# Slot tiles of a mixture-of-experts stage: probability folded into the rows, a fused ReLU and sum, more transposes by DMA, rows loaded further ahead

## The chip, the cores and the metric

The kernel runs on one core of one Trainium2 chip, as one launch. The time is the device time in microseconds; what is compared is the median over runs of the same program.

## What is computed

The input is 2 x 2048 rows of 512 float32 features. Two layers follow, each with a residual: cross-attention to 128 context rows and a quantised feed-forward in the first; a second cross-attention and a mixture of experts in the second. Only the last part is touched by the change:

```python
def _L1_ffn_ref(x, Wg, bg, We, be):      # x: layer-normalised rows
    probs = jax.nn.softmax(x @ Wg + bg, axis=-1)          # 512 columns
    idx = jnp.argmax(probs, axis=-1)
    p = jnp.take_along_axis(probs, idx[..., None], axis=-1)[..., 0]
    e_idx = idx % We.shape[0]                              # one of 8 experts
    h = jax.nn.relu(jnp.einsum('bsd,edf->besf', x, We) + be[None, :, None, :])
    onehot = jax.nn.one_hot(e_idx, We.shape[0], dtype=x.dtype)
    out = jnp.einsum('besf,bse->bsf', h, onehot) * p[..., None]
    return out
...
    x = x + _L1_ffn_ref(_layernorm(x, axis=-1), ...)
```

Each row goes to one expert, is multiplied with that expert's 512 x 512 weights, passes a ReLU, is scaled by its probability p and added to the row it came from. Since p is positive, p times the ReLU of a value is the ReLU of p times the value.

## The kernel before

The 4096 rows are 32 tiles of 128. The second layer runs a software pipeline over the tiles, `for n in range(NT)`: scores, exponentials, mixing, projection, then the gate's logits and the pick of an expert (`logits`, `picked`, `gated`, two tiles behind). `gated` leaves in each row of `xw[n]`, besides the 512 features, four columns: the mean (column D), the inverse deviation (D+1), the probability (D+2, written at L1008) and a zero (D+3). Then it writes the whole row to `x_dram`.

For the experts the rows are sorted: `routing` counts how many rows go to each expert and gives every row a place in a slot tile, 128 rows that all belong to one expert. There are 39 slot tiles. The first routing covers the first 22 row tiles and makes slot tiles 0 to 14; the second covers the rest and makes 15 to 38. `routing` is a generator whose steps are spread between other work. The second has eleven steps: one with three small products on TensorE, three of small VectorE work (the fourth the longest), two that make one-hot tables, four VectorE products of 128 x 1024 (L1124), and a last one in which TensorE sums 32 products (L1132) and VectorE turns the sums into row numbers (up to L1138).

For slot tile j, `expert(j)` does in order: start the indirect gather of tile j+4 on GpSimd (`gathered`, L1149, into one of six row buffers); turn tile j+1 (`turned_x2`); the matmuls with the expert's weights, which a register picks (L1185); normalise tile j+3 (`centered_x`, VectorE, L104); ReLU times p on ScalarE (L1188); add the row on VectorE (L1189); indirect scatter to the output on GpSimd (L1190).

There are two ways to turn a tile. On TensorE: four transposes into PSUM (L116), then a ScalarE copy that adds RAISE to one row through a bias (L1175). By DMA: VectorE adds RAISE to four columns (L1161), splits the float32 words into 16-bit halves (L826), a DMA on SP's queue transposes them (L829), and ScalarE joins the halves (`joined`, L832). RAISE carries the expert's bias into the product, since the weights hold the bias divided accordingly. Before, the odd tiles from 5 on go by DMA, 17 of 39.

From the second layer on, the order on TensorE, VectorE, ScalarE and GpSimd is the order of the program text; each engine runs its list strictly in turn. Slot tiles 0 and 1 run within the last two rounds of the attention loop, 2 to 4 between the last gate steps, 5 to 38 in the last loop, into which the steps of the second routing are woven for the first of them. PSUM tiles of the tag "m" have four buffers. All scatters write to the same output tensor.

Buffers of the slot stage are old row tiles seen through `part(n, ...)`.

Of the kernel before, what the change touches and what calls it, by code (L numbers as in the profile page):

```python
# [16 lines left out]
U16 = mybir.dt.uint16  # L17
I8 = mybir.dt.int8
AF = mybir.ActivationFunctionType
# [44 lines left out]
def two_layers(ctx: ExitStack, tc: tile.TileContext, a, out):  # L64
# [38 lines left out]
    def center(dst, x, mean, scale):  # L103
        nc.vector.tensor_scalar(dst, x, mean, scale, ALU.subtract, ALU.mult)  # L104
# [720 lines left out]
    def split(x, planes):  # L825
        nc.vector.tensor_copy(  # L826
            planes.rearrange("p (h f) -> p h f", h=2), x.bitcast(U16).rearrange("p (f h) -> p h f", h=2)
        )
        nc.sync.dma_start(out=x.bitcast(U16).rearrange("p (b q) -> p b q", q=P), in_=planes, transpose=True)  # L829

    def joined(dst, x):
        nc.scalar.copy(  # L832
            dst.bitcast(U16).rearrange("p c (q h) -> p h c q", h=2),
            x.bitcast(U16).rearrange("p (h c q) -> p h c q", h=2, c=ND),
        )
# [181 lines left out]
    def part(n, shape, dtype=F32, at=0):  # L1017

        size = math.prod(shape)
        v = xw[n][:, at : at + (size * mybir.dt.size(dtype) + 3) // 4]  # L1020
        if dtype is not F32:
            v = v.bitcast(dtype)[:, :size]
        if len(shape) == 1:
            return v
        names = "abc"[: len(shape)]
        return v.rearrange(f"p ({' '.join(names)}) -> p {' '.join(names)}", **dict(zip(names, shape)))
# [120 lines left out]
    def gathered(j):  # L1147
        if j < NJ:
# [2 lines left out]
                in_offset=bass.IndirectOffsetOnAxis(ap=tile_of[j][2], axis=0),  # L1151
            )

    def centered_x(j):
        if j < NJ:
            x = xw[j % 6]
            xn = part(6 + j % 3, [D])
            center(xn, x[:, :D], x[:, D : D + 1], x[:, D + 1 : D + 2])
            if by_dma(j):
                first = xn.rearrange("p (c q) -> p c q", c=ND)[:, :, 0:1]  # L1160
                nc.vector.tensor_scalar(first, first, RAISE, None, ALU.add)  # L1161
                split(xn, part(24 + j // 2 % 2, [2 * D], U16))

    def by_dma(j):

        return j > 4 and j % 2 == 1

    def turned_x2(j):
        if j < NJ and by_dma(j):
            ring[j] = part(9 + j % 3, [ND, P])  # L1170
            joined(ring[j], part(6 + j % 3, [D]))
        elif j < NJ:
            pt = transposed(psm, part(6 + j % 3, [D]))
            ring[j] = part(9 + j % 3, [ND, P])
            nc.scalar.activation(ring[j], pt, AF.Identity, bias=raised)  # L1175

    def expert(j):

        te, tok, _ = tile_of[j]
        gathered(j + 4)  # L1180
        turned_x2(j + 1)
        e = nc.tensor.value_load(te, min_val=0, max_val=NE - 1)
        pz = psm.tile([P, D], F32, name="pz", tag="m")
        for c in range(ND):
            nc.tensor.matmul(pz, ring[j][:, c, :], we[:, bass.ds(e, 1), c, :], start=(c == 0), stop=(c == ND - 1))  # L1185
        centered_x(j + 3)
        x, acc = xw[j % 6], part(12 + j % 3, [D])
        nc.scalar.activation(acc, pz, AF.Relu, scale=x[:, D + 2 : D + 3])  # L1188
        nc.vector.tensor_tensor(acc, acc, x[:, :D], ALU.add)  # L1189
        nc.gpsimd.indirect_dma_start(  # L1190
            out=out_rows, out_offset=bass.IndirectOffsetOnAxis(ap=tok, axis=0),
            in_=acc, in_offset=None, bounds_check=NT * P - 1, oob_is_err=False,
        )
# [32 lines left out]
    for n in range(NT):  # L1226
        blk, t = n // NB1, n % NB1
        ahead = blk + 1 < nblk
        fs = range(t * ND // NB1, (t + 1) * ND // NB1)
        if n > 0:  # L1230
            biased(n - 1)
        firsts = [m for m in (n + 2 * NB1, n + 2 * NB1 + 1) if m < NT and (m >= TURNED) == (m > n + 2 * NB1)]
        firsts = [normed(m) for m in firsts]
        scores(n)
        if 4 <= n < 4 + 2 * NE and n % 2 == 0:

            nc.scalar.dma_start(out=rowadd, in_=v_dram[(n - 4) // 2].partition_broadcast(P))

        late = t == 0 and n > 1
        if ahead and not late:  # L1240
            queries(blk + 1, fs[:1])
        if late:
            logits(n - 2)
        exponentials(n)
        if ahead and late:
            queries(blk + 1, fs[:1])
        if n == 0:
            for i in range(NT - held, NT - held + 2):
                down(i)
                widened(i + 2)  # L1250
        shares(n, 0)
        if n > 1:
            if not late:
                logits(n - 2)
            picked(n - 2)
        shares(n, 1)
        if n > 0:
            projected(n - 1)
            normed2(n - 1)()
        firsts = [first() for first in firsts]  # L1260
        rest = gated(n - 2) if n > 1 else None
        if n + 1 < NT:
            kept_keys(n + 1)
        for first in firsts:
            if first:
                first()
        if 0 < n <= NE:
            load(we[:, n - 1], a["L1_ffn_We"][n - 1].rearrange("(c p) f -> p c f", p=P))
        if ahead:
            queries(blk + 1, fs[1:])  # L1270
        if n == 0:
            for i in range(NT - held + 2, NT):
                down(i)
            dwn.close()
            ffd.close()
            moe = ctx.enter_context(tc.tile_pool(name="moe", bufs=1, side="right"))
            we = moe.tile([P, NE, ND, D], F32, name="we")
        if 4 <= n < 4 + 2 * NE:
            e, half = divmod(n - 4, 2)
            for c in range(2 * half, 2 * half + 2):  # L1280
                nc.gpsimd.tensor_tensor(we[:, e, c, :], we[:, e, c, :], rowadd, ALU.add)
        if not ahead:

            expert(n - NT + NB1)
        turned(n)
        if rest:
            rest()
        if n > 0:
            turned2(n - 1)
        mixed(n)  # L1290
        if t == NB1 - 1 and blk + 2 < nblk:
            for t in range(NB1):
                turned1((blk + 2) * NB1 + t)
        if n == NTA + 2:
            route = routing(True)
        if route:
            for _ in range(3 if n == NTA + 2 else 2):
                if next(route, route) is route:
                    route = None
                    for j in range(4):  # L1300
                        gathered(j)
                    break
        if n == NT - NB1 - 1:
            for j in range(3):
                centered_x(j)
            turned_x2(0)
    biased(NT - 1)
# [11 lines left out]
    expert(4)  # L1319
    route = routing(False)  # L1320
    for j in range(5, NJ):
        for _ in range({5: 1, 6: 2, 7: 1, 11: 1}.get(j, 2)):
            next(route, None)
        expert(j)
    sched.close()
# [40 lines left out]
```

## Time and profile before

| what | value |
|---|---|
| median of three runs | 1602.42 us (1600.16 to 1602.53) |
| the profiled execution | 1603.67 us |
| span of the profile | 1601.9 us |
| PE busy | 1553.0 us, 97% of the span |
| PEld busy | 908.7 us, 57% |
| DVE busy | 1192.1 us, 74% |
| ACT busy | 719.7 us, 45% |
| POOL busy | 583.7 us, 36% |
| slot-tile matmuls, first to last start | 1411.4 to 1591.3 us |

PE is TensorE, PEld its weight loads, DVE VectorE, ACT ScalarE, POOL GpSimd, SP the engine that issues plain DMAs. A busy share is over the whole span, which holds six stages with different limits; a stage is read from its own stretch. A float32 matmul appears as two instructions, so a slot tile has eight. The end of a matmul is modelled in the profile, so the distance between starts says more than its busy time. The chain that ended last is nearly empty here, since it only reaches back over the last scatters.

### The profile page before, as it was taken

What the parts mean: (1) busy time and instruction counts of PE and PEld (TensorE: products, weight loads), DVE (VectorE), ACT (ScalarE), POOL (GpSimd) and SP (SyncE); (2) the same over time, 40 slices, a digit from 0 to 9 for tenths busy, and PEclk for the clock granted to TensorE, in tenths of its full rate; (3) what the DMA queues carried; (4) which work ended last, traced back from release to release, by engine and by line L of the source; (5) the groups of instructions that cost most, each with busy time, mean ns of one, the idle gap of its engine ahead of it and who ended that gap; (6) DMA issues with size and microseconds to landing.
All of it is one profiled execution on the core that took longest, in us unless ns stands there. A gap on an engine that the chain in (4) does not pass through costs nothing. (4 is left out here: it accounts for less than half of the span.)

```text
span 1601.9 us, 26167 instructions
## 1 busy us (share of the span) xinstructions
PE 1553.0 (97%) x9542; PEld 908.7 (57%) x9542; DVE 1192.1 (74%) x2336; ACT 719.7 (45%) x1537; POOL 583.7 (36%) x576
## 2 busy tenths in 40 slices
PE   7999999999999999999999999999999998999997
PEld 5655555555555555544444466666666665654443
DVE  3467777777777885689986678888888889867442
ACT  1222222222222222243335566777777766753342
POOL 2232222222222222110005653556555443544553
PEclk9999999999999999999999999999999999999999
DMA  9511212111111220467668735112211121114563
GB/s 326 182 37 41 47 40 47 40 47 42 54 41 40 67 52 1 125 176 196 182 171 279 261 140 144 34 47 38 50 47 34 40 36 32 41 47 133 159 161 88
DMA packets 180571, 150.90 MB, mean 94 GB/s; under 512 B 97089, under 2 KB 144665, under 8 KB 180444
## 3 DMA queue, kind: packets, MB, share of 16 engines
q1 hardware_dynamic: 170188, 127.25, 28.7%
q0 software_dynamic: 6240, 18.70, 3.9%
q10 hardware_dynamic: 4016, 3.29, 0.9%
q8 instruction: 76, 1.25, 0.3%
q14 instruction: 51, 0.42, 0.1%
HBM read 89.97 MB, written 41.79 MB: 82 GB/s over the span
## 5 line engine op out<-in xcount | busy, mean ns | idle before, releaser
L419 ACT ACTIVATE pr<-sc 128x1024 f32<-128x1024 f32 x64 | 65.6, 1024 | 421.6 <-PE sc L414 421.4
L393 PE MATMUL pq<-xnT,wq 128*128 128x256 f32 x1024 | 254.4, 391 | 0.0
L451 PE MATMUL pw<-wo,att 128*128 128x512 f32 x512 | 230.8, 593 | 0.0
L393 PEld LDWEIGHTS pq<-xnT,wq 128*128 128x128 f32 x1024 | 184.4, 189 | 67.1 <-issue 44.4
L914 ACT ACTIVATE s<-s,mx 128x128 f32<-128x128 f32 x512 | 175.3, 388 | 31.1 <-DVE mx L905 31.0
L923 POOL TENSOR_TENSOR s<-s,rs 128x1024 f32<-128x1024 f32 x64 | 120.9, 1903 | 151.5 <-DVE rs L922 151.1
L403 POOL TENSOR_TENSOR q<-rt,rt 128x256 f32<-128x256 f32 x64 | 46.8, 731 | 339.7 <-DVE rt L402 335.2
L451 PEld LDWEIGHTS pw<-wo,att 128*128 128x128 f32 x512 | 96.9, 190 | 96.4 <-issue 89.9
L441 DVE RECIPROCAL rd<-sc 128x256 f32<-128x256 f32 x64 | 112.4, 1757 | 46.6 <-PE sc L435 46.4
L1185 PE MATMUL pz<-we,x 128*128 x312 | 140.3, 602 | 2.3 <-ACT x L832 2.0
L872 PE MATMUL pq<-xT,wq 128*128 128x256 f32 x512 | 122.6, 382 | 0.0
L978 PE MATMUL pl<-wgate,xnT 128*128 128x512 f32 x256 | 116.7, 599 | 0.0
L955 PE MATMUL pw<-wo,oT 128*128 128x512 f32 x256 | 115.2, 592 | 0.7 <-ACT oT L946 0.7
L872 PEld LDWEIGHTS pq<-xT,wq 128*128 128x128 f32 x512 | 96.0, 190 | 33.1 <-issue 20.3
L398 DVE TENSOR_TENSOR rt<-pq,rope_cos 128x256 f32<-128x256 f32 x64 | 27.0, 422 | 104.2 <-PE pq L393 104.2
L749 ACT ACTIVATE gate<-pg,gsc 128x512 f32<-128x512 f32 x88 | 60.5, 687 | 93.2 <-PE pg L744 81.8
L1185 PEld LDWEIGHTS pz<-we,x 128*128 128x128 f32 x312 | 58.2, 192 | 70.3 <-issue 66.0
L92 DVE BATCH_NORM_STATS2 st<-x 128x6 f32<-128x512 f32 x130 | 89.3, 687 | 6.0 <-DMA x<-in_ctx 3.8
L744 PE MATMUL pu<-xqT,wuT 128*128 128x512 bf16 x352 | 90.3, 379 | 2.1 <-DVE h L752 2.0
L744 PE MATMUL pg<-xqT,wgT 128*128 128x512 bf16 x352 | 90.3, 379 | 0.0
L900 DVE SCALAR_TENSOR_TENSOR s<-sc,keep 128x1024 f32<-128x1024 f32 x64 | 78.0, 1219 | 13.4 <-PE sc L892 7.7
L810 PE MATMUL py<-wdT,hb 128*128 128x512 bf16 x352 | 78.9, 384 | 2.3 <-DVE hb L804 1.5
(221 smaller groups left out, 2777.9 us busy)
## 6 DMA issues: line engine op xcount, KB each, us to landing
h_dram<-h SPq DMA_DIRECT2D x88, 256.0 KB
hq<-h_dram SPq DMA_DIRECT2D x31, 704.0 KB
x_dram<-x SPq DMA_DIRECT2D x32, 258.0 KB
x<-in_x SPq DMA_DIRECT2D x32, 256.0 KB
we<-in_L_ffn_We SPq DMA_DIRECT2D x8, 1024.0 KB
xnT<-in_x_turned SPq DMA_DIRECT2D x14, 512.0 KB
along<-stat_dram SPq DMA_DIRECT2D x14, 256.0 KB
w_in<-in_L_ffn_w_gate SPq DMA_DIRECT2D x11, 256.0 KB
```

Source lines behind the costliest of these rows:

```text
L92: nc.vector.bn_stats(out=st, in_=x)
L393: nc.tensor.matmul(pq, wqs[c // 2][:, c % 2, par, g * P : (g + 1) * P], xnTs[k][:, c, :], start=(c == 0), stop=(c == ND - 1))
L441: nc.vector.reciprocal(rd, sc[:, 0, B0:])
L451: nc.tensor.matmul(pw, atts[u][:, f, t * P : (t + 1) * P], wo[:, 2 * g + f, :], start=(g == 0 and f == 0), stop=(g == NG - 1 and f == 1),)
L744: nc.tensor.matmul(dst, w[:, c, i * P : (i + 1) * P], xqTs[blk][:, c, :], start=(c == 0), stop=(c == ND - 1),)
L810: nc.tensor.matmul(py, hbs[n][:, i, :], wdT[:, i, :], start=(i == 0), stop=(i == NI - 1))
L872: nc.tensor.matmul(pq, wq1[:, c, f * P : (f + 1) * P], xTs[blk][:, c, :], start=(c == 0), stop=(c == ND - 1))
L914: nc.scalar.activation(s[:, h, :], s[:, h, :], AF.Exp, bias=mx[:, h : h + 1], **accum)
L923: nc.gpsimd.tensor_tensor(s, s, rs.unsqueeze(2).to_broadcast([P, 8, T]), ALU.mult)
L955: nc.tensor.matmul(pw, os_[n][:, c, :], wo1[:, c, :], start=(c == 0), stop=(c == ND - 1))
L978: nc.tensor.matmul(pl, xn2T[n][:, c, :], wgate[:, c, :], start=(c == 0), stop=(c == ND - 1))
L1185: nc.tensor.matmul(pz, ring[j][:, c, :], we[:, bass.ds(e, 1), c, :], start=(c == 0), stop=(c == ND - 1))
```

## The change

Four things change. The inverse deviation is multiplied by p (into column D+3) before the rows are normalised, and the raised columns get p times RAISE, so that the product comes out scaled by p. ReLU and the addition of the row become one VectorE operation that reads PSUM; it stands ahead of the normalising of a later tile, which before stood ahead of the addition. Of the tiles from 5 on, those not divisible by three go by DMA: 23 of 39. Gathers and normalising run one tile further ahead (j+5 and j+4), with a fourth buffer for normalised rows; five gathers and four normalised tiles precede the slot tiles, and the second routing is stepped so that it ends ahead of slot tile 10, where it ended ahead of slot tile 11.

```diff
@@ -1151,42 +1151,46 @@
                 in_offset=bass.IndirectOffsetOnAxis(ap=tile_of[j][2], axis=0),
             )
 
+    def xn_of(j):
+        return part((6, 7, 8, 26)[j % 4], [D])
+
     def centered_x(j):
+
         if j < NJ:
-            x = xw[j % 6]
-            xn = part(6 + j % 3, [D])
-            center(xn, x[:, :D], x[:, D : D + 1], x[:, D + 1 : D + 2])
+            x, xn = xw[j % 6], xn_of(j)
+            p = x[:, D + 2 : D + 3]
+            rp = x[:, D + 3 : D + 4]
+            nc.vector.tensor_tensor(rp, x[:, D + 1 : D + 2], p, ALU.mult)
+            center(xn, x[:, :D], x[:, D : D + 1], rp)
+            first = xn.rearrange("p (c q) -> p c q", c=ND)[:, :, 0]
+            nc.vector.scalar_tensor_tensor(first, p.to_broadcast([P, ND]), RAISE, first, ALU.mult, ALU.add)
             if by_dma(j):
-                first = xn.rearrange("p (c q) -> p c q", c=ND)[:, :, 0:1]
-                nc.vector.tensor_scalar(first, first, RAISE, None, ALU.add)
-                split(xn, part(24 + j // 2 % 2, [2 * D], U16))
+                split(xn, part(24 + j % 2, [2 * D], U16))
 
     def by_dma(j):
 
-        return j > 4 and j % 2 == 1
+        return j > 4 and j % 3 > 0
 
     def turned_x2(j):
-        if j < NJ and by_dma(j):
+        if j < NJ:
             ring[j] = part(9 + j % 3, [ND, P])
-            joined(ring[j], part(6 + j % 3, [D]))
-        elif j < NJ:
-            pt = transposed(psm, part(6 + j % 3, [D]))
-            ring[j] = part(9 + j % 3, [ND, P])
-            nc.scalar.activation(ring[j], pt, AF.Identity, bias=raised)
+            if by_dma(j):
+                joined(ring[j], xn_of(j))
+            else:
+                nc.scalar.copy(ring[j], transposed(psm, xn_of(j)))
 
     def expert(j):
 
         te, tok, _ = tile_of[j]
-        gathered(j + 4)
+        gathered(j + 5)
         turned_x2(j + 1)
         e = nc.tensor.value_load(te, min_val=0, max_val=NE - 1)
         pz = psm.tile([P, D], F32, name="pz", tag="m")
         for c in range(ND):
             nc.tensor.matmul(pz, ring[j][:, c, :], we[:, bass.ds(e, 1), c, :], start=(c == 0), stop=(c == ND - 1))
-        centered_x(j + 3)
         x, acc = xw[j % 6], part(12 + j % 3, [D])
-        nc.scalar.activation(acc, pz, AF.Relu, scale=x[:, D + 2 : D + 3])
-        nc.vector.tensor_tensor(acc, acc, x[:, :D], ALU.add)
+        nc.vector.scalar_tensor_tensor(acc, pz, 0.0, x[:, :D], ALU.max, ALU.add)
+        centered_x(j + 4)
         nc.gpsimd.indirect_dma_start(
             out=out_rows, out_offset=bass.IndirectOffsetOnAxis(ap=tok, axis=0),
             in_=acc, in_offset=None, bounds_check=NT * P - 1, oob_is_err=False,
@@ -1297,11 +1301,11 @@
             for _ in range(3 if n == NTA + 2 else 2):
                 if next(route, route) is route:
                     route = None
-                    for j in range(4):
+                    for j in range(5):
                         gathered(j)
                     break
         if n == NT - NB1 - 1:
-            for j in range(3):
+            for j in range(4):
                 centered_x(j)
             turned_x2(0)
     biased(NT - 1)
@@ -1319,7 +1323,7 @@
     expert(4)
     route = routing(False)
     for j in range(5, NJ):
-        for _ in range({5: 1, 6: 2, 7: 1, 11: 1}.get(j, 2)):
+        for _ in range(1 if j == 7 else 2):
             next(route, None)
         expert(j)
     sched.close()
```

`center(dst, x, mean, scale)` is one VectorE operation, (x - mean) times scale, with one value per partition for each. `transposed` is the four TensorE transposes.

## What the change will do to the time

> **What bounds the kernel now.** I read the table by stage first, then the groups of the stretch with the slot tiles, then one engine at a time in order of time. M(j) is the eight matmul instructions of slot tile j (L1185), T(j) its four transposes (L116). The stage table gives the stretch, then busy time and count of PE, PEld, DVE, ACT and POOL, the granted clock, the DMA share and GB/s.
>
> ```profile
> 1460.00:1480.00 20.00, 20.00 (x56) 9.11 (x55) 16.95 (x43) 7.17 (x9) 9.62 (x10) 1.00 0.56 153
> 1480.00:1500.00 20.00, 17.73 (x74) 8.41 (x73) 10.37 (x20) 7.78 (x9) 10.27 (x10) 0.91 0.57 149
> 1560.00:1580.00 20.00, 19.45 (x54) 8.90 (x53) 8.35 (x17) 8.77 (x11) 10.08 (x10) 1.00 0.56 155
> ```
>
> Until 1480 us TensorE has no gap, and VectorE is nearly full with the second routing. At 1480 TensorE pauses. After 1500 no engine looks short of time, TensorE least of all; but its busy time is modelled, so I measured the pitch. When nothing holds it back, T and two M take 7.31 us (T starts at 1465.33 and 1472.63 in the PE timeline), a matmul start every 0.43 us: M is 3.44, T 0.43. From 1561.62 to 1584.78 a pair takes 7.72. Something else sets the pace there. POOL in order of time (start, duration, what it is, idle before and its releaser):
>
> ```profile
> 1503.62 1.02 POOL L1190 DMA_INDIRECT out_x<-x,x  x1 [1.38 <-DVE x L1189]
> 1504.94 0.98 POOL L1149 DMA_INDIRECT x<-x_dram,x  x1 [0.30 <-ACT x L1188]
> 1507.63 1.02 POOL L1190 DMA_INDIRECT out_x<-x,x  x1 [1.71 <-DMA out_x<-x,x]
> 1508.96 1.10 POOL L1149 DMA_INDIRECT x<-x_dram,x  x1 [0.30 <-ACT x L1175]
> 1511.18 1.02 POOL L1190 DMA_INDIRECT out_x<-x,x  x1 [1.12 <-DVE x L1189]
> ...
> 1515.44 1.02 POOL L1190 DMA_INDIRECT out_x<-x,x  x1 [1.96 <-DMA out_x<-x,x]
> ```
>
> Each scatter waits until the one before has landed. Asked one at a time, those at 1507.63 and 1515.44 land after 2.7 and 2.8 us, the one at 1511.18, beside a DMA transpose, after 3.5; the next starts about 0.8 us after a landing. So scatters cannot follow closer than about 3.5 us, or 4.0 beside a transpose, and from 1499.94 to 1580.75 they stand 3.85 us apart. The gathers queue behind them on POOL, and each gather holds VectorE's next centering:
>
> ```profile
> L1190 POOL DMA_INDIRECT out_x<-x,x x39 | 41.3, 1058 | 62.4 <-DVE x L1189 32.0 <-DMA out_x<-x,x 21.8 <-issue 3.2
> L104 DVE TENSOR_SCALAR x<-x 128x512 f32<-128x512 f32 x39 | 22.6, 583 | 56.6 <-DMA x<-x_dram,x 56.2 <-PE pid L1132 0.5
> L832 ACT COPY x<-x 128x1024 uint16<-128x1024 uint16 x17 | 22.8, 1340 | 24.7 <-DMA x<-x 13.0 <-DVE x L1189 7.4 <-DVE x L104 3.2
> ```
>
> In these groups (busy, mean ns, idle before and releasers) the 56.2 us is a ring: centering, add, scatter, gather, the centering two tiles on. At 1501.20, 1508.46 and 1515.90 it took 7.26 and 7.44 us a turn, from 1570.40 to 1578.38 7.98.
>
> The pause at 1480 is TensorE waiting for the routing's four one-hot products (L1124) on VectorE:
>
> ```profile
> 1479.94 0.56 PE L1132 MATMUL pid<-x,x 128*128 128x48 bf16 x16
> 1481.89 0.37 PE L1132 MATMUL pid<-x,x 128*128 128x48 bf16 x8 [1.39 <-DVE x L1124]
> 1483.02 0.37 PE L1132 MATMUL pid<-x,x 128*128 128x48 bf16 x8 [0.76 <-DVE x L1124]
> 1483.24 0.64 PE L116 MATMUL pt<-ident,x 128*128 128x128 f32 x4
> ```
>
> **The fused operation.** 39 ScalarE ReLUs (684 ns) go; the add (685 ns) becomes one VectorE operation reading PSUM. No row is that operation; L956, an addition from PSUM of the same shape, takes 665 and L821, a fused form from SBUF, 751. I take 0.69; ends 0.66 and 0.75. VectorE gains per tile the product of two columns (0.15 to 0.2, as L963 and L100) and the raising of four columns, now on all 39 tiles rather than 17 (0.2, L1161). From start to start a DMA tile costs VectorE 0.62 + 0.19 + 0.57 + 0.20 + 0.61 = 2.19 us (1.98 before), a PE tile 1.5 (1.06 before). Against a pitch near 3.6 that is covered everywhere except in the routing. At the end it shows fully: last matmul to last scatter is 1591.9 to 1593.64 now, ReLU, add and 0.3 of handover; one of the two goes: **-0.7**.
>
> **Sixteen tiles transposed on TensorE in place of 22.** Each T removed frees 0.43. From T(12) on, 14 become 9. The six new DMA transposes each add a 0.7 us split, 1.23 us of issue on SP and a 1.34 us ScalarE copy (L832). ScalarE lost its ReLU, and SP issues nothing else here. From SP's issue to the copy's start took 3.4 us at 1502.88 and 4.2 at 1510.10. The Trainium skill, VectorE: DVE Perf Modes, Rules for kernel authors, says to transpose 128x128 on TensorE where a PSUM destination will do. By that rule the six should stay, forgoing 2.6 us in all; the row says that a T costs the engine with the work 0.43 while the DMA form runs beside it, so I follow the row, and charge its real price, the collisions, below.
>
> **Rows a tile further ahead.** The fused operation now stands ahead of the centering, so it no longer waits behind a gather. The ring spans three tiles: 0.7 + 0.3 + 1.3 + up to 4.5 for the gather (the longest between 1495 and 1582) + 1.6 is 8.4 us, against 10.7 of TensorE work (three M and one T). It stops binding. What is late next is the scatter chain, which this edit leaves. On VectorE the centering waits behind the fused operation, and that behind M(j); split, transpose and copy then need 2.5 + 4.2 + 1.4 = 8.1 us of the 10.7 until M(j+4).
>
> In the attention loop the fifth gather (0.95, plus 0.3) pushes L949 and then L923 by 0.65 at 1395, with 0.7 free before the transposes need it; four centerings at 1401 instead of three and their small operations put L900 back about 1.2, with 1.0 free at 1414.9. ScalarE gets 0.7 back per slot tile there. I take **+0.2**, ends -0.6 and +0.7.
>
> **Routing one tile sooner.** This is the loss. Its eleven steps now end ahead of M(10), not M(11). VectorE runs them in order with the tiles' work. I add from 1457.55, the end of M(4), from start to start with before's rows: fused and DMA centering of tile 8, 2.19; steps 1 and 2, 0.5 + 1.75; from there five fused at 0.62; a PE tile 0.9, steps 3 and 4, 3.94; a DMA tile 1.57, step 5, 1.67; a DMA tile, steps 6 and 7, 1.41 + 1.13; a PE tile, two products, 2.27; a DMA tile and the last product, 1.2. That ends at 1483.1, where before's ended at 1482.96, with one M fewer done. M(5) starts at 1458.35 as now, so M(9) ends five M and one T later, at 1476, and TensorE idles for most of 7 us; M(10) starts at 1483.4. Ends 1482.5 and 1485.5, the latter with every fused operation 0.4 longer.
>
> The Trainium skill, TensorE: Matmul & The Clock Gate, Part 1: The HAM clock gate, speaks against this: an idle window of about 3.4 us halves the clock, and a busy window restores it. The trace agrees:
>
> ```profile
> 1484.50:1488.00 3.50, 3.50 (x6) 1.40 (x5) 2.04 (x7) 0.16 (x1) 2.04 (x3) 0.51 0.80 216
> ```
>
> Two pauses of 1.39 and 0.76 us cost one half-clock window, 1.7 us. By the row a new pause costs the same; by the rule it starts somewhere inside a window and costs 0.85 to 2.6, the mean again 1.7. I take 1.7.
>
> **Sum.** Before, from 1483.24: 28 M and 14 T, 102.3 us; the last matmul ends at 1591.9, 6.2 later than work plus 0.2 of pipeline: 1.7 clock, 4.5 waiting. After, from 1483.4: 29 M and 9 T, 103.6, +0.2, +1.7: 1588.9 if nothing else holds TensorE; last scatter 1.0 later, 1589.9. A scatter beside a transpose (4.0) lags the 3.58 pitch until it has slipped some 2.4 us past the transposes' packets; the last four tiles land in 2.1 (the scatter at 1590.43) and recover most of it; I leave 1.0. Thus 1590.9 against 1593.64, **-2.7**, with the early +0.2 **-2.5**. The profiled execution took 1603.67: 1601.2. The median shown is 1.25 lower: 1599.9. I add 0.5, because an execution of before need not have had its half-clock window at the routing, and after surely has: **1600.4 us**.
>
> **Rivals.** *Faster:* no lag (-1.0), a 0.85 clock loss (-0.85) and no early cost (-0.2): 1598.4. For it: with the fused operation ahead of the split, the scatter's packets leave about 1 us before the transpose's. Against: any slip brings them together.
>
> *Slower:* the scatter chain takes the ring's place. Two tiles in three have a transpose beside the scatter. If all slip to 4.0, with M(10)'s scatter at 1489.8, 24 of them reach 1585.8 and four emptier ones (4.0 + 3 x 2.9) 1598.5, 4.9 later than now: 1607.3. It decides above a mean pitch of 3.80, where the end is today's. For it: the chain already paces before. Against: the 2.7 us rows when no transpose is near.
>
> *No change:* the VectorE walk is 2 us short, M(10) starts at 1485.4: 1602.4.
>
> **Numbers.** Likeliest 0.41, faster rival 0.31, slower rival 0.16, longer routing 0.12. About 0.2%, 3.2 us, is what can be told from no change: the bounds are 1599.2 and 1605.6. The likeliest's own range, 1598.8 to 1602.5, gives 0.06 to faster; the rest of it and most of the longer routing are no change: 0.37 faster, 0.46 same, 0.17 slower. Range 1597 to 1606.
>
> **What would show it.** Right: TensorE idle between about 1476 and 1483 ahead of L1132, then one half-clock stretch; later, three M and one T in 10.7 to 10.9 us; L104's wait for the gathers gone. Wrong: L1190 still waiting on its own DMA with a pitch of 3.8 or more, or L832 on transposes.

## The result and the profile after

The changed kernel takes **1611.29 us**, the median of six runs (1607.44 to 1612.33), beside 1600.89 for the kernel before in the same rounds: 1.0061 times as long, with an interval of 1.0051 to 1.0071. The forecast was 1600.4 with a range up to 1606, and "no change" as the likeliest. It is slower, by about 10 us.

The stage table of the changed kernel (stretch; busy time and count of PE, PEld, DVE, ACT, POOL; granted clock, DMA share, GB/s):

```profile
1460.00:1480.00 20.00, 18.63 (x58) 8.60 (x56) 18.65 (x55) 5.47 (x7) 10.33 (x10) 1.00 0.68 172
1480.00:1500.00 20.00, 14.82 (x52) 7.15 (x53) 9.60 (x21) 2.95 (x3) 7.46 (x8) 0.74 0.48 108
...
1560.00:1580.00 20.00, 18.47 (x46) 7.92 (x45) 9.88 (x24) 4.47 (x4) 10.32 (x10) 1.00 0.69 167
```

VectorE is fuller before 1480 (18.65 beside 16.95), TensorE has nearly 3 us less work in the next 20 us and a mean clock of 0.74 instead of 0.91, and near the end TensorE again has holes. TensorE in order of time around the second routing's end (start, duration, what, idle before and its releaser):

```profile
1472.42 6.17 PE L1190 MATMUL pz<-we,x 128*128 x14
1478.43 0.36 PE L1132 MATMUL pid<-x,x 128*128 128x48 bf16 x8
1480.86 0.37 PE L1132 MATMUL pid<-x,x 128*128 128x48 bf16 x8 [2.07 <-DVE x L1124]
1482.00 0.50 PE L1132 MATMUL pid<-x,x 128*128 128x48 bf16 x8 [0.76 <-DVE x L1124]
1485.31 0.50 PE L1132 MATMUL pid<-x,x 128*128 128x48 bf16 x8 [2.81 <-DVE x L1124]
1486.55 6.52 PE L1190 MATMUL pz<-we,x 128*128 x8 [0.74 <-issue]
1492.90 0.60 PE L116 MATMUL pt<-ident,x 128*128 128x128 f32 x4
1493.34 1.02 PE L1190 MATMUL pz<-we,x 128*128 x2
```

The forecast pause is there, from 1478.5 to 1486.5, and behind it M(10) takes 6.8 us to the start of M(11) where M and T need 3.87: the clock is at one half from 1482.0 to 1492.3. One stretch out of the middle of that, by the stage table:

```profile
1488.00:1491.50 3.50, 3.50 (x5) 1.35 (x4) 0.00 (x0) 0.00 (x0) 0.00 (x0) 0.50 0.27 76
```

The groups that answer to those of before, over the whole profile:

```profile
L1194 POOL DMA_INDIRECT out_x<-x,x x39 | 41.4, 1061 | 68.3 <-DMA out_x<-x,x 18.0 <-DVE x L1192 16.5 <-DVE x L1163 16.2
...
L832 ACT COPY x<-x 128x1024 uint16<-128x1024 uint16 x23 | 30.8, 1341 | 69.0 <-DMA x<-x 50.7 <-DVE x L1166 9.1 <-DVE x L1090 4.3
...
L104 DVE TENSOR_SCALAR x<-x 128x512 f32<-128x512 f32 x39 | 22.5, 577 | 2.7
```

L104's idle time before it fell from 56.6 to 2.7 us. Most of the fall is only a change of name: the product p times inverse deviation (L1163) now stands first and takes the wait for the gather. From 1495 on:

```profile
L1163 DVE TENSOR_TENSOR x<-x 128x1 f32<-128x1 f32 x24 | 3.8, 159 | 34.4 <-DMA x<-x_dram,x 34.4
```

But from 1493.34 to 1561.21 TensorE keeps exactly its own pace, 10.74 us for three M and one T (M(11) at 1493.34, M(14) at 1504.08), so the ring holds TensorE up no more until then. And yet nothing is won. GpSimd in order of time, the gathers left out, first behind the routing and then at the end:

```profile
1508.12 1.01 POOL L1194 DMA_INDIRECT out_x<-x,x  x1 [2.75 <-DMA out_x<-x,x]
...
1511.80 1.01 POOL L1194 DMA_INDIRECT out_x<-x,x  x1 [1.39 <-DMA out_x<-x,x]
...
1515.38 1.01 POOL L1194 DMA_INDIRECT out_x<-x,x  x1 [1.29 <-DVE x L1192]
...
1519.38 1.01 POOL L1194 DMA_INDIRECT out_x<-x,x  x1 [1.70 <-DVE x L1192]
...
1593.44 1.00 POOL L1194 DMA_INDIRECT out_x<-x,x  x1 [2.77 <-DMA out_x<-x,x]
1596.31 0.98 POOL L1194 DMA_INDIRECT out_x<-x,x  x1 [1.87 <-issue]
1599.17 0.98 POOL L1194 DMA_INDIRECT out_x<-x,x  x1 [1.88 <-DMA out_x<-x,x]
1602.02 0.98 POOL L1194 DMA_INDIRECT out_x<-x,x  x1 [1.86 <-issue]
```

The releaser named in the brackets misleads. The landings, read one at a time, are 2.87, 2.77 and 3.19 us after the starts at 1508.12, 1511.80 and 1515.38, and each next scatter starts 0.81 us after the landing: 1515.38 + 3.19 + 0.81 = 1519.38, though the row names VectorE. From slot tile 12 to the last, every link of the changed kernel is of this kind. Before, from 12 to 34, 16 of 23 were; the other seven started 0.1 to 0.5 us later, 1.8 us together. So in **both** kernels the tail is set by one chain, scatter after scatter, of a landing and 0.8 us each. All that the ring and TensorE added to it before was these 1.8 us and, at the last scatter, which waited for the last tile's sum, 0.35. TensorE's last matmul ends at 1597.16, 4.9 us ahead of the last scatter; before, it was 1.7.

M(j) is the eight matmul instructions of slot tile j; let SC(j) be its scatter. Then the profiled executions differ like this (us, before and after):

| stretch | before | after | difference |
|---|---|---|---|
| start of M(0) | 1411.44 | 1411.63 | +0.19 |
| M(0) to M(5), attention loop and gate steps | 46.91 | 49.12 | +2.21 |
| M(5) to M(11), routing | 25.64 | 32.59 | +6.95 |
| M(11) to SC(11) | 7.12 | 4.61 | -2.51 |
| SC(11) to SC(38), the chain | 102.53 | 104.07 | +1.54 |
| last scatter | 1593.64 | 1602.02 | +8.38 |

The third and fourth row belong together: before, M(11) itself ran under the half clock (5.2 us). The chain starts 6.8 us late and hands all of it to the end. The other 0.3 us up to the executions' difference of 8.66 (1603.67 to 1612.33) lies behind the last scatter. The medians differ by 10.4: the profiled execution of before was 2.8 us above its median, that of the change 1.0, so 1.7 us of the loss are not located by this table.

### The profile page after: what moved, and what is told of

Its sections match the earlier page's. It is cut to its first block, busy times and chain, and to the rows that moved or that the text cites. A ratio compares the mean times of both kernels' runs of the same rounds, so it can differ in the third digit from the quotient of the medians.

```text
span 1610.5 us, 26109 instructions
## 1 busy us (share of the span) xinstructions
PE 1549.8 (96%) x9518; PEld 906.0 (56%) x9518; DVE 1207.7 (75%) x2403; ACT 698.6 (43%) x1498; POOL 580.0 (36%) x576
```

## The experiments

Times are medians, ratios stand against the kernel before on the same chip. Four chips were used for them; the kernel before took 1600.1, 1600.8 and 1601.3 us on three of them, 1603.2 and 1605.2 on the fourth, so runs on different chips are compared by their distance from it. From the trace of one execution: the start of the chain as SC(13) - M(0), the mean distance of the scatters from 13 to 34, and SC(38) - M(0), all in us. These executions lie between 3.2 us below and 5.1 us above the median of their run, so a difference of a few us in the last three columns proves nothing alone. A and B are the two theories that each expectation sets against each other. The rows are grouped as the text takes them up; "mended" is explained with its group.

| run | time | ratio, interval | SC(13)-M(0) | distance | SC(38)-M(0) |
|---|---|---|---|---|---|
| before | 1600.89 | | 88.50 | 3.85 | 182.19 |
| changed | 1611.29 | 1.0061 (1.0051-1.0071) | 96.49 | 3.88 | 190.38 |
| changed again | 1613.44 | 1.0077 (1.0054-1.0099) | 95.69 | 3.95 | 191.20 |
| changed, two targets | 1605.98 | 1.0037 (1.0023-1.0050) | 93.64 | 3.58 | 182.99 |
| before, two targets | 1599.08 | 0.9986 (0.9980-0.9992) | 86.76 | 3.72 | 178.06 |
| before, routing sooner | 1604.93 | 1.0025 (1.0017-1.0032) | 90.49 | 3.85 | 184.08 |
| changed, routing later | 1610.84 | 1.0072 (1.0046-1.0098) | 93.84 | 3.94 | 189.13 |
| changed, kept warm | 1617.85 | 1.0099 (1.0085-1.0114) | 93.77 | 4.31 | 196.67 |
| changed, ReLU early | 1610.68 | 1.0080 (1.0055-1.0105) | 93.93 | 3.87 | 187.77 |
| changed, ReLU early, again | 1611.01 | 1.0058 (1.0045-1.0071) | 94.76 | 3.95 | 190.32 |
| before + fused alone | 1606.17 | 1.0029 (1.0020-1.0037) | 89.04 | 4.02 | 186.39 |
| before, two of three by DMA | 1607.70 | 1.0024 (1.0012-1.0036) | 88.59 | 4.15 | 190.92 |
| changed, alternate by DMA | 1611.58 | 1.0069 (1.0055-1.0083) | 93.19 | 3.96 | 188.30 |
| mended | 1609.08 | 1.0047 (1.0033-1.0062) | 84.72 | 4.31 | 187.75 |
| mended, two targets | 1601.16 | 0.9985 (0.9978-0.9991) | 88.11 | 3.77 | 181.49 |
| mended, alternate | 1606.95 | 1.0024 (1.0017-1.0031) | 88.70 | 3.90 | 182.63 |
| mended, none by DMA | 1607.68 | 1.0030 (1.0018-1.0041) | 88.64 | 3.93 | 185.01 |
| before, DMA later | 1601.28 | 1.0003 (0.9992-1.0013) | 85.56 | 3.90 | 180.14 |
| before, split later | 1604.73 | 1.0001 (0.9993-1.0009) | 87.18 | 3.91 | 182.05 |

**Is the chain of scatters the limit of the tail?** The odd slot tiles are scattered to a tensor of their own, so that a scatter waits only for the one before the last; their rows are missing from the output, so this kernel only measures.

```diff
+    odd_rows = dram.tile([NT * P, D], F32, name="odd_rows")
...
-            out=out_rows, out_offset=...
+            out=odd_rows if j % 2 else out_rows, out_offset=...
```

> The changed kernel, with the rows of odd slot tiles scattered to a scratch tensor instead of the output, so that a scatter waits for the one two tiles back; the odd tiles' rows are missing from the output. Theory A (the chain of scatters to one tensor paces the tail): the changed kernel's scatters stand 3.98 us apart from slot tile 10 (1494.1) to 34 (1589.7) while three M and one T take 10.7; with two targets the last scatter follows the last matmul by 1 us instead of 5, and TensorE's 3.6 us of waits after 1561 go: about 7.5 us less than the changed kernel, near 1604. Theory B (the whole loss is TensorE's pause at the routing with its slow clock; the scatters only follow): at most 1 us less, 1610 to 1612.

5.9 us above the kernel before on its chip, where the change is 10.4 above: about 4.5 us less, not the 7.5 of A, though the trace from M(0) to the end is 7.4 shorter. The last scatter is 1.0 us behind the last matmul, TensorE has no gap to the end, and the scatters are 3.58 us apart, which is its pace. From 1495 on the waits of the scatters for DMA are nearly gone, and so is the product's wait for the gathers, 1.4 us for 34.4:

```profile
L1195 POOL DMA_INDIRECT out_x<-x,x x15 | 16.0, 1065 | 26.8 <-DVE x L1164 17.4 <-DVE x L1193 7.5 <-DMA odd_rows<-x,x 1.9
L1195 POOL DMA_INDIRECT odd_rows<-x,x x14 | 15.0, 1070 | 19.2 <-DVE x L1193 9.1 <-DVE x L1164 8.3 <-DMA out_x<-x,x 1.9
L1191 PE MATMUL pz<-we,x 128*128 x223 | 97.2, 592 | 0.0
L1164 DVE TENSOR_TENSOR x<-x 128x1 f32<-128x1 f32 x24 | 3.8, 157 | 1.4 <-DMA x<-x_dram,x 1.4
```

So the chain is the limit of the changed tail. The same edit in the kernel before:

> The kernel before the change, with the rows of odd slot tiles scattered to a scratch tensor, so that a scatter waits for the one two tiles back; the odd tiles' rows are missing from the output. Theory A (the chain of scatters paced the tail before the change too, which is why the change could not shorten it): the slot tiles close up from 3.85 us to about TensorE's 3.65, 24 of them save 4 to 5 us: 1595 to 1597. Theory B (before the change the ring of centering, add, scatter, gather set the pace, and the chain of scatters only followed): the ring stays, 1 us less at most: 1599 to 1600.

1.7 us less by the medians, 0.14% by the ratio, and by the trace 4.1 us from M(0) to the end. The size lies between A and B; the mechanism is A's. From 1495 on:

```profile
L1186 PE MATMUL pz<-we,x 128*128 x205 | 90.2, 593 | 0.0
L104 DVE TENSOR_SCALAR x<-x 128x512 f32<-128x512 f32 x23 | 13.3, 578 | 36.7 <-DMA x<-x_dram,x 34.6 <-PE pz L1186 2.1
```

The ring is still there, for L104 waits 34.6 us for gathers, but TensorE has no gap at all: M(14) to M(38) take 87.9 us, where 24 M and 12 T take 87.7. So the chain was the limit before too. The ring held TensorE up only through it, since each gather stands behind a scatter in GpSimd's list; next in line is TensorE's own pace.

**What does the earlier end of the routing cost?** In the kernel before, one line:

```diff
-        for _ in range({5: 1, 6: 2, 7: 1, 11: 1}.get(j, 2)):
+        for _ in range(1 if j == 7 else 2):
```

> The kernel before the change with only the second routing stepped as in the changed one, so that it ends ahead of slot tile 10. Theory A (the earlier end of the routing alone makes TensorE pause for 6 us ahead of tile 10, costs half-clock windows, and lets the chain of scatters restart late): tile 13's scatter comes 4 to 6 us later than in the kernel before, and the whole run with it: 1604 to 1606. Theory B (the pause of the changed kernel comes from the heavier VectorE work per slot tile, not from the schedule): 2 us more at most, 1600 to 1602.

+4.1 us. TensorE in order of time (as above):

```profile
1477.93 0.37 PE L1132 MATMUL pid<-x,x 128*128 128x48 bf16 x8 [0.86 <-DVE x L1124]
1479.06 0.37 PE L1132 MATMUL pid<-x,x 128*128 128x48 bf16 x8 [0.76 <-DVE x L1124]
1481.26 0.50 PE L1132 MATMUL pid<-x,x 128*128 128x48 bf16 x8 [1.82 <-DVE x L1124]
1482.07 5.94 PE L1185 MATMUL pz<-we,x 128*128 x8 [0.31 <-issue]
```

The pause comes a tile earlier with a tile less done, and the half clock lasts 6.8 us here, not 3.4. The distance of the scatters is unchanged at 3.85. A holds by the time; by the trace the chain starts only 2.0 us later, not 4 to 6, so half of the price is not located in the traces.

The other way round, in the changed kernel the routing is put back to end ahead of M(11), with the gather of tile 15 held back to match:

```diff
-        for _ in range(1 if j == 7 else 2):
+        for _ in range({5: 1, 6: 2, 7: 1, 11: 1}.get(j, 2)):
...
-        gathered(j + 5)
+        if j + 4 == NJA:
+            gathered(NJA)
+        if j + 5 != NJA:
+            gathered(j + 5)
```

> The changed kernel, with the second routing stepped as before the change, so that it ends ahead of slot tile 11; only the gather of tile 15 moves to the start of tile 11. Theory A (the pause ahead of tile 10 delays both TensorE and the chain of scatters, which restarts at 1494.1): M(11) starts near 1486.5 instead of 1493.3 and the chain runs on from tile 9 without its 11 us hole; the end is then set by 24 scatters of 3.95 us and the last four: 7 to 9 us less, 1602 to 1604. Theory B (the tail is paced by the chain of scatters wherever TensorE pauses, and the routing only moves idle time about): 2 us less or nothing, 1609 to 1611.

B: no gain that can be told, though the chain starts 2.7 us earlier by the trace. The head start did not reach the end. To take away only the half clock, five idle-filling float32 products (no one reads them) go between the groups of the routing's sums:

```diff
+            for _ in range({8: 2, 24: 3}.get(n, 0) if dm is not None else 0):
+                nc.tensor.matmul(dm, ident, wq1[:, 0, :], start=True, stop=True)
```

> The changed kernel with five matmuls more, whose result nothing reads, put between the groups of eight products at the end of the second routing, where TensorE would wait for VectorE. Theory A (the pause also costs half-clock windows, 10.2 us long, 5.7 of them with slot tile matmuls running, which are worth 2.9 us): the clock stays whole, slot tile 10 takes 3.4 us instead of 6.8, and the end comes 2 to 3 us sooner than the changed kernel's. Theory B (the end is set by the chain of scatters alone): within 1 us of the changed kernel.

Neither. The clock stays whole, M(10) takes 3.97 us to M(11), and TensorE reaches M(13) 2.5 us sooner, counted from M(5). But the run is not faster: its median is 4.4 us *above* that of the change on the same chip. With four runs against six, and ratios whose intervals overlap, that it is slower is not shown. Its stage table:

```profile
1480.00:1500.00 20.00, 17.59 (x73) 7.80 (x72) 12.41 (x26) 3.75 (x4) 8.41 (x8) 1.00 0.57 132
1560.00:1580.00 20.00, 15.27 (x41) 6.82 (x40) 7.92 (x21) 4.88 (x5) 8.57 (x10) 1.00 0.58 136
```

The clock is 1.00 where the change has 0.74, and eighty microseconds later TensorE has 41 instructions in 20 us instead of 46: the scatters land after 3.5 us in the mean instead of 3.07 and stand 4.31 apart, and TensorE, out of buffers, waits for them. What TensorE gains ahead of the tail did not reach the end, and in this trace, the slowest of the four executions, the chain itself was slower.

**What does the fused operation cost where VectorE is full?** In the changed kernel ReLU and addition are two operations again for slot tiles 0 and 1, which run inside the attention loop:

```diff
-        nc.vector.scalar_tensor_tensor(acc, pz, 0.0, x[:, :D], ALU.max, ALU.add)
+        if j < 2:
+            nc.scalar.activation(acc, pz, AF.Relu)
+            nc.vector.tensor_tensor(acc, acc, x[:, :D], ALU.add)
+        else:
+            nc.vector.scalar_tensor_tensor(acc, pz, 0.0, x[:, :D], ALU.max, ALU.add)
```

> The changed kernel, with ScalarE's ReLU and a VectorE addition for slot tiles 0 and 1 alone, those inside the attention loop. Theory A (a PSUM buffer is freed late: the fused operation stands in VectorE's list behind the next normalisation, and the fourth transpose of the probabilities waits for the buffer, 1.4 us at 1417.9 and 0.8 a round later): both waits go, slot tile 2 starts 2.2 us sooner, and so does everything after it: 2.2 us less, near 1609. Theory B (the early loss comes from the four normalised tiles and five gathers put ahead of the slot tiles): 0.5 us at most, near 1611.

Its time could not be told from the change (single runs spread to 1622), so it was repeated beside a second measurement of the changed kernel:

> The changed kernel itself, as the base for the other three on the same chip: 10 us over the kernel before, as it was.

> The changed kernel with ScalarE's ReLU for slot tiles 0 and 1, timed beside the changed kernel on the same chip. Theory A (the two waits for the PSUM buffer delay everything after them): 2 to 2.5 us less than the changed kernel. Theory B (the chain of scatters, which paces the tail, absorbs them): within 0.7 us of it.

The medians of this pair differ by 2.4 us, as in A. But single runs of the changed kernel lie between 1608.88 and 1621.78, the intervals of the two ratios overlap, and the first run lay 10.6 us above the kernel before where the change lies 10.4: a gain at the end is not shown. At the front it is: M(0) to M(5) is 46.8 us in both traces, and 49.1 in all six traces of the changed kernel that have the fused operation from tile 0 and DMA transposes from tile 5. TensorE behind M(0), first in the changed kernel, then in the first of these runs:

```profile
1415.07 1.47 PE L116 MATMUL pt<-ident,s 128*128 128x128 f32 x12
1417.94 0.66 PE L116 MATMUL pt<-ident,s 128*128 128x128 f32 x4 [1.40 <-DVE x L1192]
```

```profile
1414.22 1.91 PE L116 MATMUL pt<-ident,s 128*128 128x128 f32 x16
```

The fourth group of transposes needs the PSUM buffer of M(0). Before, ScalarE's ReLU began to read it at 1415.08; the fused operation stands in VectorE's list and starts at 1417.20, and TensorE waits 1.40 us, and 0.83 at the same place one round later. The operation is not slower than the addition (687 ns beside 685); the buffer is held by its place in a longer list.

The fused form alone, in the kernel before (p in the rows, fused operation first; lead, routing and choice of tiles as before):

> The kernel before the change with only the probabilities in the normalised rows and the fused operation ahead of the normalising; every other tile by DMA, rows, routing and gathers as before. Theory A (PSUM freed late in the attention loop, about 2 us, and a longer VectorE list beside the routing, about 2 us, are costs of the fused operation itself): 3 to 5 us over the kernel before. Theory B (the costs come from the sooner routing and the further transposes alone, and the ring of the gathers that this order dissolves even gains): 1 us over it or less.

+4.9 us, A: M(0) to M(5) is 1.8 longer, the routing's last sum, counted from M(5), 1.1 later. The scatters stand 4.02 apart although no transpose was added, but this trace is the slowest of twelve executions.

**What do more transposes by DMA cost?** In the kernel before, and then back to alternate tiles in the changed one:

```diff
-        return j > 4 and j % 2 == 1
+        return j > 4 and j % 3 > 0
```

> The kernel before the change with two of three tiles by DMA from tile 5 on, and nothing else. Theory A (six more transposes lengthen the chain of scatters, and six more splits VectorE's list): tiles 13 to 34 stand 3.95 us apart or more in place of 3.85, 2 to 5 us more than before: 1603 to 1606. Theory B (what a transpose taken from TensorE saves, 0.43 us each, shows): up to 2.5 us less, 1598 to 1601.

> The changed kernel with every other tile transposed by DMA as before the change, in place of two of three. Theory A (a DMA transpose beside a scatter makes it land later, and the chain of scatters paces the tail): scatters come down from 3.98 to about 3.8 us apart, 24 of them save 4 us, less what TensorE's five transposes more cost where it is short of time: 3 to 5 us less, 1606 to 1608. Theory B (TensorE is the bound after the pause): 5 transposes of 0.43 us more, 2 us more, near 1613.

In the kernel before, +0.24%, scatters 4.15 apart (in an execution 4.0 us above the median): A. In the changed kernel, taking the six away again wins nothing (distance 3.96): neither. So the six transposes are a cost, but not one that lies on top of the others.

**If the front is mended, does the tail gain appear?** "Mended" is the changed kernel with ReLU apart for tiles 0 and 1, the routing later, and no transpose by DMA before tile 14 (`j > 13 and j % 3 > 0`).

> The changed kernel with ScalarE's ReLU for slot tiles 0 and 1, the second routing stepped as before the change (the gather of tile 15 at the start of tile 11), and DMA transposes only from tile 14 on, so that VectorE makes no splits (0.6 us each, four of them) beside the routing. Theory A (VectorE's list paces everything up to the end of the routing, and the chain of scatters carries the delay to the end): 2.4 us from the attention loop, about 5 from the routing with fewer half-clock windows: 1602 to 1605. Theory B (what costs is the tail with two of three transposes by DMA): only the 2.4 us, near 1609.

The time is B's. By the trace the front is better than in either kernel: the chain starts at 84.72 us, 3.8 ahead of the kernel before, with no half clock. The run is still 0.47% slower than before: from SC(13) to SC(38) it takes 103.0 us, 9.1 more than the changed kernel, at a distance of 4.31. Its POOL rows show how:

```profile
1543.16 1.37 POOL L1201 DMA_INDIRECT out_x<-x,x  x1 [1.48 <-DVE x L1166]
...
1549.27 1.02 POOL L1201 DMA_INDIRECT out_x<-x,x  x1 [3.26 <-DMA out_x<-x,x]
...
1552.79 1.02 POOL L1201 DMA_INDIRECT out_x<-x,x  x1 [1.23 <-DMA out_x<-x,x]
```

One link takes 6.1 us, the next 3.5. Three variants of it, with two targets for the scatters, with alternate tiles, and with no DMA transposes in this stage (`return False`):

> The mended changed kernel (ScalarE's ReLU for tiles 0 and 1, routing stepped as before, DMA transposes from tile 14 on), with the rows of odd slot tiles scattered to a scratch tensor; these rows are missing from the output. In the mended kernel tile 13's scatter stood 10 us sooner after slot tile 5 than in the changed one, yet the scatters of tiles 13 to 34 then stood 4.31 us apart in place of 3.88 and gave it back. Theory A (the chain of scatters to one tensor is what gives it back): with two targets they stand 3.6 us apart, the end comes 10 us or more sooner: 1595 to 1599. Theory B (the gathers or the DMA transposes themselves are late, the scatters only follow): above 4.0 us apart still, 1605 to 1608.

> The mended changed kernel with every other tile from 15 on by DMA, in place of two of three. Theory A (a scatter beside a DMA transpose lands late; fewer transposes, shorter chain): scatters 3.8 us apart in place of 4.31, 10 us less than the mended kernel, 1598 to 1601. Theory B (the share of transposes does not matter for the pace of the scatters, as between the changed kernel and its alternate form): above 4.1 us apart, 1606 to 1609.

> The mended changed kernel with every slot tile transposed by TensorE. Theory A (the DMA transposes are what makes scatters land late): every scatter lands in 2.6 to 2.8 us, TensorE with four transposes per tile is the bound at 3.87 us a tile, and the last scatter follows the last matmul by 1 us: 1601 to 1604. Theory B (scatters land late without transposes too, beside the gathers): above 4.0 us apart, 1606 or more.

With two targets it is 0.15% *below* the kernel before: A, the chain is what gave it back. Alternate tiles are 0.24% above, neither A nor B, but below the 0.47 of two tiles in three with intervals apart: fewer transposes help here. Without DMA the last scatter is 1.0 us behind the last matmul and the matmuls stand 3.87 apart, TensorE's own pace for M and T: it has become the bound, as A says, but costs more than A's time; this trace does not tell the landings. The traces of these three hold a stall of some 4 us between slot tiles 1 and 2 that the mended kernel's doesn't, so their third and fifth columns are that much too large: ScalarE's copy of the mixed values (L946) is late, TensorE waits 2.54 us there and not 0.67, and a stretch at half clock follows. The cause is open, but it goes with the chip: the two other traces from it ("two of three by DMA" and "split later") have 1.78 and 1.68 us at this place, all fourteen others 0.67 or 0.68, and the kernel before is slowest on it. If the stall is in every execution, an estimated 3 us of these three times belong to it, 4.2 less the 1.1 to 1.3 of the other two.

And in the kernel before, no DMA transposes until tile 14, first alone, then with gathers and centering one tile further ahead and the split left where it was:

> The kernel before the change with DMA transposes only from tile 15 on (every other tile), so that tiles 5 to 13 are transposed by TensorE and VectorE makes no splits beside the routing. Theory A (the routing's VectorE list sets when the tail starts): three splits and raisings of 0.9 us less, the routing ends 2.7 us sooner, TensorE pauses less and keeps its clock; 2 to 4 us less than before, 1596 to 1598. Theory B (TensorE's four transposes more, 1.7 us, eat it up, or the chain of scatters hides it): within 1 us of the kernel before.

> The kernel before the change with the split of a tile, and so its DMA transpose, moved one tile behind its normalising (after the next centering, which waits for a gather), rows one tile further ahead to make room for it, the gather of tile 15 at the start of tile 11, and DMA transposes from tile 15 on. Theory A (a scatter lands late when a DMA transpose is issued from 2 us before it to 1 us after it): transposes are now issued some 2 us after a scatter starts, scatters of tiles 13 to 34 land in 2.8 us on average in place of 2.95, and stand 3.7 us apart in place of 3.85: 2 to 4 us less than before, 1597 to 1599. Theory B (the ring of gather and centering holds the pace of 3.85 anyway): within 1 us of the kernel before.

B for both. The chain starts 2.9 and 1.3 us sooner, the half clock at the routing is gone, and no difference in time can be told. In the second the transposes were meant to leave at another point of the scatter; they came to lie mostly 0.7 to 1.2 us ahead of one again, so it does not test that. No run that writes every row is faster than the kernel before.

## Why the prediction was wrong

Its sum for the last scatter was 1591.1 us (1590.9 and the early 0.2). It came at 1602.02, 10.9 later.

- **The pause: right.** The walk along VectorE's list gave M(10) 25.05 us behind M(5); it took 25.80 (0.75 more). The walk itself was nearly exact: the last product on VectorE ended 24.50 us behind M(5), where it had put 24.75 (its terms add up to 1483.2, not 1483.1). One half-clock stretch was named as the loss.
- **Clock, mis-sized.** "I take 1.7"; it cost 2.9. (+1.2) The prediction priced it by before's two short pauses, 3.41 us of half clock. The new pause holds gaps of 2.07, 0.76, 2.81 and 0.74 us, and half clock lasted 10.24 us, three times 3.41, 5.7 of it with M(10) running. TensorE's busy time in four stretches of 3.41 us, the first ending where the clock falls:

```profile
1478.61:1482.02 3.41, 0.58 (x17) 0.36 (x13) 3.27 (x7) 1.35 (x1) 2.10 (x2) 1.00 0.57 172
1482.02:1485.43 3.41, 0.60 (x11) 0.46 (x12) 3.13 (x6) 0.00 (x0) 1.33 (x1) 0.50 0.47 140
1485.43:1488.85 3.42, 2.68 (x11) 1.43 (x11) 0.62 (x4) 0.00 (x0) 0.97 (x1) 0.50 0.59 114
1488.85:1492.26 3.41, 3.41 (x5) 1.35 (x4) 0.00 (x0) 0.00 (x0) 0.00 (x0) 0.50 0.14 54
```

Each of the first three was followed by one at half clock; only the full one brought the clock back. In the repeat of the change a stretch 87% busy did, half clock lasted 6.83 us, and M(10) lost 1.6; in the six traces of the changed kernel with this routing and no filling products it lost 1.6 to 3.1. The Trainium skill, TensorE: Matmul & The Clock Gate, Part 1: The HAM clock gate, which the prediction weighed, has the length of the stretch, but speaks of an idle window of about 3.4 us. Here no gap was longer than 2.81, and in before the clock fell after a stretch with 1.77 us busy; the measurement decides. Read by that page, the loss would be the rest of the window in which TensorE starts again and one full window, an estimate of 1.7 to 3.4 us. The prediction's "0.85 to 2.6" counted half a window too few.

- **Early cost, mis-sized.** "+0.2, ends -0.6 and +0.7" was 2.4. It counted instruction times on VectorE and GpSimd, and credited ScalarE with 0.7 per tile. It did not ask who frees PSUM: moving the read of PSUM from a short list to a long one made TensorE wait 1.40 and 0.83 us for a buffer, and with ReLU apart M(0) to M(5) is 2.35 us shorter. (+2.2) The costs that it did count, the gathers and the normalised tiles ahead of M(0), show as +0.19 there; as M(0) starts anywhere from 1409.7 to 1414.5 in the traces, that this fits the +0.2 is luck.
- **Tail: the step that failed.** "4.5 waiting" were to vanish because the ring stops binding, with 1.0 of lag left and a drain 0.7 shorter; from M(11) to the last scatter 101.9 us were forecast and 108.7 measured. (+6.8) Three M and one T do take 10.74, up to 1561; L104's wait for gathers did go, though mostly to L1163. So all its signs of being right came in, and its sign of being wrong too: the scatters still wait for their own landings, 3.88 us apart. The ring was not what set the end: with two targets and the ring in place, TensorE in before has no gap from 1495 on. The scatters' own 3.85 was read in the profile, and the prediction said itself that the change leaves this chain; it then put the chain's floor at 3.5 to 4.0 and let it lag by 1.0 us only. It forgot that a chain that is the limit also passes on every delay of its start: the drain is void, since the last scatter now waits for the one before it and not for a matmul (before, the last sum had put it off by 0.35), and TensorE's shorter work is void for the same reason.

The rival "slower" had the right mechanism, the chain in the ring's place, but its mean of 4.0 is not what happened; the distance is 3.88, and the loss came from a chain that starts 6.8 us late. Its chance of 0.16 was too small: before, other waits than the chain's own had put off its scatters by 1.8 us in all, so removing them could not be worth 4.5. The advice that the prediction set aside, to leave the six transposes on TensorE, was right in the kernel before, where moving them cost 0.24%; in the changed kernel moving them back won nothing.

The separate prices, 4.1 (routing), 4.9 (fused form), 3.9 by its ratio (six transposes), add up to 12.9, more than the 10.4 that the change costs. Likely they overlap in the same chain, for taking the routing or the transposes back alone won nothing; reading the rows one tile further ahead has no run of its own. Why scatters land later once TensorE runs ahead of them is not settled. Landing times go with the transposes: those of tiles 13 to 33 with a DMA transpose issued between 2.2 us ahead of the scatter's start and 1.2 us after it take 3.20 us in the mean (10) before and 3.26 (14) in the change, the others 2.73 (11) and 2.70 (7). In the kept-warm run the first kind has 3.85, in the mended one 3.88. That is a correlation; no run moved the transposes clear of the scatters with all else the same.

## What to carry to other kernels

Where writes to one tensor must land one after the other, measure the links (landing plus restart) and compare their distance with the engines' own pace before anything else: while such a chain is the limit, work removed from engines beside it is worth nothing, and a late start of it can reach the end in full, as here; an earlier start did not always. When an operation that frees a buffer moves to another engine, look at its place in that engine's list, not at its duration. And when two limits lie close together, price the removal of one by the gap to the other.

## What the runs showed of the hardware that was not expected

- An indirect scatter of 128 rows landed after 2.1 us when only scatters were left, about 2.7 with gathers around it, and 3.2 beside a DMA transpose. Over the twelve traces with one target that tell the landings (tiles 13 to 33), where the transpose was issued up to 0.5 us after the scatter's start it took 3.3 to 4.9 us, 4.5 in the mean (7 cases); where none was issued from 2.2 us ahead of the start to 2 us after it, 2.8 in the mean (100 cases, one as long as 5.0).
- Filling TensorE's pause with five products held the clock at 1.00 and won no time.
- Pauses that look alike cost differently: gaps of 1.39 and 0.76 us were followed by 3.4 us of half clock, of 0.86, 0.76 and 1.82 by 6.8, of 2.07, 0.76 and 2.81 by 10.2, and, in the repeat of the change, of 2.11, 0.76 and 2.94 by 6.8. Ahead of the kernels' last microseconds, half clock came in multiples of 3.41 us.
